# A two-layer kernel with an order written by a planner: 40 instead of 42 dense chunks ahead of the routing, and gathered rows added five steps behind their request

## The chip, the cores and the metric

The kernel runs on one core of one Trainium2 chip. Engines are called PE (TensorE, matrix products; PEld is its weight load), DVE (VectorE), ACT (ScalarE), POOL (GpSimd) and SP (SyncE, which here only issues DMAs). The metric is the device time of one execution in microseconds, as the median of several runs. Everything is computed in 32-bit floats.

## The reference

Four sequences of 512 tokens with 256 features (2048 tokens) go through two layers. Each layer normalises x, and adds an attention-like and a feed-forward branch to x.

```
xn = layernorm(x)
x  = x + attn0(xn) + ffn0(xn)
     attn0: q, k, v = xn Wq, xn Wk, xn Wv (+ biases);  phi = elu + 1
            ((phi(q) * cumsum(phi(k) * v)) / 4) Wo + bo           # sum along the sequence
     ffn0:  logits over 512 genes, top 32, softmax, weighted mean of gene vectors,
            tanh(mean Wd) * rms(xn) * (mean Wu) * 0.1
xn = layernorm(x)
x  = x + attn1(xn) + ffn1(xn)
     attn1: q, k, v = rms(xn) Wqkv;  q, k = rms(q), rms(k);  w = exp(k)
            y = sigmoid(q) * cumsum(w * v) / (cumsum(w) + 1e-6)
            xn + (u * silu(g)) Wout   with u, g = y Wswiglu      # width 1024
     ffn1:  16 experts of width 176, top 2 by softmax, weighted;
            plus a shared expert of width 352
```

## The kernel before

**Stages.** (1) The *planned stage*, 0 to 295 us: all of layer 0 and, in layer 1, everything up to `y` and the router's choice. It works in five *units*: the two halves of batch 0 (units 0 and 1, 256 tokens each), then batches 1, 2 and 3 (units 2, 3 and 4, 512 tokens each). (2) *Routing*: `route` works out, for each token and choice, the row (`slot`) at which the token is stored for its expert, then `scatter` writes the tokens' rows to `xrows` in device memory by 32 indirect DMAs of POOL. (3) The *expert stage*, 363 to 463 us: 19 pairs of 128-row tiles are fetched, turned, multiplied with their expert's weights (`up_tile`, `down_pair`) and stored to `yrows`. (4) The *last stage*: the rows of each token are gathered back by 32 indirect DMAs of POOL (L1610), multiplied with the choice's weight and added to x by DVE (L1621), and x is stored.

**Dense chunks.** The rest of layer 1 (the product of `y` with the wide weights, and the shared expert) is filler for TensorE, cut into 88 *chunks*: 8 halves of a batch (256 tokens), each with 11 blocks of hidden units (3 of the shared expert, 8 of attention). A chunk is an up product into a PSUM tile `gu` (L1163), a tanh on ACT (`th`), two multiplications that make `hid`, and a down product that adds to `acc` (L1184), which has a single buffer. After a half's last block `sum_up` (L1196, DVE) adds `acc` to x and so frees it. Chunks `0 .. UPTO-1` run in the planned stage, five beside `route`, 18 beside `scatter`, three more before the experts, and all others in the last stage. There the down product of a chunk follows the up product of the one two later (`behind`). Each indirect DMA is *paced*: it waits for the latest down product (`beat`).

**The planner.** In the planned stage the order of instructions of PE, DVE, ACT and POOL is not that of the program text. Work is written as generators that yield what they need next: an engine with an estimated duration, a buffer (`take`, `give`), or an event (`wait`, `post`). `Order.run` keeps a clock for each engine and picks among the steps that could begin within `PULL[engine]` of the earliest the one with the lowest rank. `RANKS` has a rank for each kind of work and unit. Each engine then executes its list in that fixed order. Outside the planned stage a scheduler orders the instructions by their place in the text and by dependences.

**Lean choices.** `LEAN` says, for each unit, which engine does a step. `rise`: whether the gene branch's product is made by ACT and POOL (L626, L629) instead of DVE (L634). `value`: whether `v` is scaled by ACT (L861) instead of DVE (L867). `begin`: whether layer 1's normalisation (L374, called from `begin_stream`) runs on POOL instead of DVE. `inverse`, of effect only in units of 512 tokens: whether one reciprocal of 256 columns (L966) serves two columns at once, with POOL multiplying before (L962) and after it (L978, L979) and the last product in the form L981 instead of L990. `dense`: chunks below this number have `hid` made by an ACT copy (L1240) and a POOL multiplication (L1243); the others by a DVE multiplication (L1246). `norm` and `taken` belong to layer 0 and are the same in both kernels.

**Chain of a unit in layer 1.** `begin_stream`: moments and factors (DVE, L361 to L371, L812 to L814), normalisation (L374), transposes (PE, L380); an addition of `xn` to x on POOL (L822). `rest_stream`: products with the weights `w1` (PE, L877), squares and exponentials (ACT), then for each of two heads of columns `gate_stream`: a transpose, a running sum (DVE, L933), the product L953, reciprocals (L966), another transpose and running sum, and the product that makes `yT` (L990 or L981). The wide chunks of a batch need its `yT`.

**The last stage's loop** steps once per chunk. The requests, the adds and the stores of it:

```
for step, _ in enumerate(dd):
    while asked < 2 * NTT and 5 * asked <= 9 * step:          # gather a row block (POOL)
    while added < 2 * NTT and 15 * added <= 32 * (step - 3):  # add one (DVE), store each fourth (SP)
```

With `NTT` = 16 there are 32 requests and 32 adds; `NT` = 4 tiles of 128 tokens make a batch.

Of the kernel before, what the change touches and what calls it, by code (L numbers as in the profile page):

```python
# [17 lines left out]
P = 128  # L18
B, L, D = 4, 512, 256
NT = L // P  # L20
# [8 lines left out]
NTT = B * NT  # L29
# [20 lines left out]
def together(*streams):  # L50
# [9 lines left out]
PE, DVE, ACT, POOL = "PE", "DVE", "ACT", "POOL"  # L60
# [1 line left out]
REACH = {PE: 0.2, DVE: 0.13, ACT: 0.15, POOL: 0.1}  # L62


PULL = {PE: 0.2, DVE: 0.02, ACT: 0.05, POOL: 0.1}

RANKS = dict(
    front=(-12, 14.5, -21, -10.5, -7.5),  # L70
    turn=(-35, -36, -36, -36.5, -31.5),
    logit=(10.5, 14, 25.5, 28, 26),
    top=(-11.5, 16, 15.5, 16.5, 26),
    gene=(-46.5, -21, -41.5, -40, -30.5),
    kv=(-2, 21.5, -7.5, -8.5, 17.5),
    q=(37.5, 43, 41.5, 50, 43),
    out=(-23.5, -22.5, -5.5, -6.5, -15),
    begin=(-23.5, -26.5, -27.5, -17.5, -15.5),
    rest=(9, -28.5, -9, 4.5, -27),
    weigh=(51.5, 51, 51.5, 50.5, 52.5),  # L80
    gate=(3.5, 4, -1.5, 4.5, 9.5),
    router=(32.5, 34, 26.5, 29, 33.5),
    dense=(49, 9.5, 2),
)


# [18 lines left out]

LEAN = dict(
    taken=(1, 0, 1, 1, 1),
    rise=(0, 0, 1, 0, 0),
    norm=(0, 1, 1, 1, 1),
    value=(1, 0, 1, 1, 0),  # L110
    inverse=(1, 1, 1, 0, 0),
    begin=(0, 1, 1, 0, 1),
    dense=27,
)


class Order:
# [67 lines left out]
    def run(self):  # L185
        while self.live:
# [6 lines left out]
            if not self.live:  # L193
# [6 lines left out]
                for j, (s, t) in enumerate(zip(ready, begin))  # L200
                if s.ask[0] == engine and t <= begin[first] + PULL[engine]
            ]
# [12 lines left out]
def tile_two_layers(  # L215
# [23 lines left out]
    nc = tc.nc  # L239
# [5 lines left out]
    xs = const.tile([P, B, NT, D], F32, name="xs")  # L245
# [911 lines left out]
    NC = len(chunks)  # L1157
# [13 lines left out]
    def source(half):  # L1171

        unit = (half // 2, half % 2 * 2)
        return (unit, 0) if unit in made else ((half // 2, 0), half % 2 * HB)
# [19 lines left out]
    def sum_up(half):  # L1194
        here = xs[:, half // 2, half % 2 * 2 : half % 2 * 2 + 2]
        V.scalar_tensor_tensor(here, acc, 0.5, here, ALU.mult, ALU.add)  # L1196

    def dense(first, behind):

        for c in range(first, 2 * B * NC):
            half, n = divmod(c, NC)
            unit, t0 = source(half)
            m = chunks[n][4]
            gu = ps_d.tile([P, 2, HB], F32, name="gu")
            up_product(gu, made[unit], t0, *chunks[n])
            th = wd.tile([P, HB], F32, name="th", bufs=3)
            S.activation(th[0:m], gu[0:m, 0], AF.Tanh, scale=0.5)  # L1209
            hid = wd.tile([P, HB], F32, name="hid", bufs=4)  # L1210
            V.scalar_tensor_tensor(th[0:m], th[0:m], 1.0, gu[0:m, 0], ALU.add, ALU.mult)  # L1211
            V.tensor_tensor(hid[0:m], gu[0:m, 1], th[0:m], ALU.mult)
            behind.append((half, n, hid))
            if len(behind) > 2:
                half, n, hid = behind.pop(0)
                down(half, n, hid)
                if n == NC - 1:
                    sum_up(half)
            yield
        for half, n, hid in behind:  # L1220
            down(half, n, hid)
        sum_up(half)
# [93 lines left out]
    def weight_stream():  # L1316
# [10 lines left out]
        for transfer in incoming:  # L1327
            paced(transfer)
            c += 1
            if c < UPTO:  # L1330
                yield "wait", ("down", c)

    UPTO = 42
    kinds = mybir.EngineType
    with tc.manual_schedule(engines={kinds.PE, kinds.DVE, kinds.Activation, kinds.Pool}):

# [15 lines left out]
        order.add(more_constants(), RANKS["front"][0])  # L1352
        dense_streams(order, UPTO)
        for unit, (b, i0, nt) in enumerate(((0, 0, 2), (0, 2, 2), (1, 0, NT), (2, 0, NT), (3, 0, NT))):
# [5 lines left out]
        order.run()  # L1360
    mixing.close()
    dd = dense(UPTO, [])

    def d(n):
# [240 lines left out]
    added = 0  # L1605
    for step, _ in enumerate(dd):
        while asked < 2 * NTT and 5 * asked <= 9 * step:
            n, k = divmod(asked, 2)
            paced(
                G.indirect_dma_start(  # L1610
                    out=ys[:, asked],
                    out_offset=None,
                    in_=yrows,
                    in_offset=bass.IndirectOffsetOnAxis(ap=slot[:, k, n : n + 1], axis=0),
                ).ins
            )
            asked += 1
        while added < 2 * NTT and 15 * added <= 32 * (step - 3):
            n, k = divmod(added, 2)
            here = xs[:, n // NT, n % NT]  # L1620
            V.scalar_tensor_tensor(here, ys[:, added], cpair[:, k, n : n + 1], here, ALU.mult, ALU.add)  # L1621
            added += 1
            if added % 4 == 0 and added < 2 * NTT:
                b, i = divmod(n - 1, NT)
                nc.sync.dma_start(
                    out[b, i * P : (i + 2) * P].rearrange("(t p) d -> p t d", p=P), xs[:, b, i : i + 2]
                )
    assert asked == added == 2 * NTT
    for i in (NT - 2, NT - 1):
        nc.sync.dma_start(out[B - 1, i * P : (i + 1) * P], xs[:, B - 1, i])  # L1630

# [54 lines left out]
```

## Time and profile before

| | us |
|---|---|
| median of 3 runs (lowest to highest) | 526.89 (526.8 to 528.15) |
| the profiled execution | 527.08 |
| its span on the core | 525.4 |

| stage of the profiled execution | from, to |
|---|---|
| planned stage, to the first product of the routing | 0 to 296.06 |
| routing, scatter, 26 dense chunks | 296 to 363 |
| experts | 363 to 463 |
| last stage, to the first of the last two stores | 463 to 520.46 |
| those stores, and the end of the program | 520.46 to 525.4 |

Busy time is a share of the span; matrix products are pipelined, so that a busy PE is not a PE at its peak, but a gap in it is time in which no product was under way. In a timeline row stand start, duration, engine, line, operation, written tile `<-` read tiles, shapes and count; in brackets the engine's idle time just before and what ended it.

### The profile page before, as it was taken

The numbers are of one execution on the slowest core, as the hardware profiler recorded it, in microseconds if no ns is written. First come the engines' busy times: TensorE is split into PE (matmuls) and PEld (weight loads), VectorE is DVE, ScalarE is ACT, GpSimd is POOL, SyncE is SP. The second block draws the span as 40 slices with busy tenths as digits, with TensorE's granted clock in tenths as the row PEclk, the third lists the DMA queues.
The fourth block names the chain that finished last, engine by engine and source line by source line (L and its number), as shares of the span: only waits on it lengthen the run. The fifth ranks groups of instructions, "written<-read, shape, count | busy, mean of one in ns | idle before, by whom it ended". The sixth has DMA issues, their size and how long they took to land.

```text
span 525.4 us, 7219 instructions
## 1 busy us (share of the span) xinstructions
PE 506.4 (96%) x2352; PEld 371.8 (71%) x2352; DVE 346.5 (66%) x938; ACT 238.0 (45%) x539; POOL 197.7 (38%) x229
## 2 busy tenths in 40 slices
PE   7899999999999999999899999999999999999895
PEld 5555575565676787678578888887776767688784
DVE  5899989999899799859559783333222222226653
ACT  2864896668757845873381111113333333311110
POOL 1713076364745566477220126660000000026562
PEclk8999999999999999999999999999999999999998
DMA  7999000000000000006516203245237345114442
GB/s 213 351 378 327 1 1 1 1 1 2 0 1 1 1 1 1 1 1 181 151 48 183 100 30 139 92 185 182 88 100 289 102 154 196 61 61 130 130 122 83
DMA packets 38920, 53.71 MB, mean 102 GB/s; under 512 B 4096, under 2 KB 33888, under 8 KB 38624
## 3 DMA queue, kind: packets, MB, share of 16 engines
q1 hardware_dynamic: 35104, 44.82, 25.2%
q0 software_dynamic: 3072, 8.39, 4.9%
q8 instruction: 20, 0.33, 0.3%
q14 instruction: 20, 0.16, 0.1%
q10 hardware_dynamic: 704, 0.01, 0.1%
HBM read 27.12 MB, written 18.61 MB: 87 GB/s over the span
## 4 chain that ended last, share of the span: by engine, by line
PE 62%; DVE 17%; POOL 8%; issue 5%; ACT 3%; DMA 2%; SPq 0%; POOLq 0%; ACTq 0%; DVEq 0%
PE gu L1163 16%; PE pu L1461 9%; PE acc L1184 8%; PE py L1483 6%; PE pm L877 6%; POOL ys L1610 5%; PE pm L413 4%; PE pt L1414 3%; PE pm L456 3%; DVE rep L560 3%; DVE top L558 2%; PE pm L380 2%; DVE sums L966 1%; PE pm L483 1%; PE pm L489 1%
## 5 line engine op out<-in xcount | busy, mean ns | idle before, releaser
L1163 PE MATMUL gu<-yT,wugt 128*128 128x256 f32 x512 | 120.4, 379 | 0.0
L1163 PEld LDWEIGHTS gu<-yT,wugt 128*128 128x128 f32 x512 | 96.3, 190 | 13.4 <-issue 0.8
L1610 POOL DMA_INDIRECT ys<-yrows,slot x32 | 30.5, 952 | 129.1 <-PE gu L1163 111.9
L1184 PE MATMUL acc<-wot,hid 128*128 128x256 f32 x256 | 66.0, 383 | 2.3 <-DVE hid L1246 1.4
L1209 ACT ACTIVATE th<-gu 128x256 f32<-128x256 f32 (+1 forms) x46 | 17.6, 383 | 103.9 <-PE gu L1163 61.6
L1184 PEld LDWEIGHTS acc<-wot,hid 128*128 128x128 f32 x256 | 47.1, 190 | 11.9 <-DVE hid L1246 2.9
L1163 PE MATMUL gu<-xn1T,sgu 128*128 128x256 f32 (+1 forms) x192 | 45.4, 380 | 0.0
L1461 PE MATMUL pu<-wex,xgT 128*128 x128 | 43.6, 463 | 1.8 <-issue 1.0
L877 PE MATMUL pm<-w,xn1T 128*128 128x512 f32 (+1 forms) x128 | 45.2, 495 | 0.0
L1211 DVE SCALAR_TENSOR_TENSOR th<-th,gu 128x256 f32<-128x256 f32 (+1 forms) x46 | 19.1, 415 | 39.1 <-ACT th L1209 27.8
L1470 DVE TENSOR_TENSOR hb<-pu,hb 128x176 f32<-128x176 f32 x38 | 13.0, 341 | 43.8 <-ACT hb L1469 43.8
L1138 POOL DMA_INDIRECT xrows<-xn,slot x32 | 31.0, 967 | 28.0 <-DVE hit L1118 11.2
L374 POOL TENSOR_SCALAR xn<-xs,mv,rs 128x256 f32<-128x256 f32 x24 | 29.3, 1233 | 27.8 <-DVE rs L754 21.1
L1163 PEld LDWEIGHTS gu<-xn1T,sgu 128*128 128x128 f32 (+1 forms) x192 | 34.5, 181 | 7.2 <-issue 1.0
L413 PE MATMUL pm<-xnT,wqkv 128*128 128x512 f32 x72 | 33.9, 598 | 0.0
L877 PEld LDWEIGHTS pm<-w,xn1T 128*128 128x128 f32 x128 | 23.5, 190 | 14.4 <-issue 10.7
L558 DVE MAX8 top<-rep 128x8 f32<-128x512 f32 x48 | 32.8, 683 | 0.3
L560 DVE MATCH_REPLACE8 rep<-top,rep 128x512 f32<-128x512 f32 x48 | 32.4, 675 | 0.0
L456 PE MATMUL pm<-wct,xnT 128*128 128x512 f32 x64 | 31.8, 620 | 0.3 <-ACT lg L517 0.2
L1474 DVE COPY hgT<-pt 128x512 f32<-128x512 f32 x19 | 13.1, 692 | 28.6 <-PE pt L1414 28.6
L1483 PE MATMUL py<-wex,hgT 128*128 x128 | 30.6, 382 | 0.0
L1233 ACT ACTIVATE th<-gu 128x256 f32<-128x256 f32 (+1 forms) x42 | 16.0, 383 | 31.9 <-PE gu L1163 30.8
(205 smaller groups left out, 946.6 us busy)
## 6 DMA issues: line engine op xcount, KB each, us to landing
xrows<-zero SPq DMA_DIRECT2D x1, 6016.0 KB
wex<-in_w_gate_up_dram SPq DMA_DIRECT2D x8, 704.0 KB, 5.0
xn<-wex SPq DMA_DIRECT2D x9, 608.0 KB, 4.3
xg<-xrows SPq DMA_DIRECT2D x19, 256.0 KB, 2.8
yrows<-yg SPq DMA_DIRECT2D x19, 256.0 KB, 2.1
wugt<-in_wug_dram SPq DMA_DIRECT2D x1, 2048.0 KB
wex<-in_w_down_dram SPq DMA_DIRECT2D x4, 512.0 KB
w<-wex SPq DMA_DIRECT2D x3, 608.0 KB
```

The lines of the kernel that those rows point to most:

```text
L374: engine.tensor_scalar(to, xs[:, b, i], mv[:, 0:1], rs[:, 0:1], ALU.subtract, ALU.mult)
L413: T.matmul(pm, wqkv[:, h, c * P : (c + 1) * P], k.xnT[:, h, tok], start=(h == 0), stop=(h == NH - 1),)
L456: T.matmul(pl, k.xnT[:, h, i * P : (i + 1) * P], wct[:, h], start=(h == 0), stop=(h == NH - 1))
L558: V.max(tp[:, 8 * r : 8 * r + 8], src)
L560: V.match_replace(rep, tp[:, 8 * r : 8 * r + 8], src, TAKEN)
L877: T.matmul(po[:, 0:n], g.xnT[:, h, i * P : (i + 1) * P], w1[:, h, 0:n] if o == "q" else w1[:, h, 2 * D : 2 * D + n], start=(h == 0), stop= ...
L1138: sc = G.indirect_dma_start(out=xrows, out_offset=bass.IndirectOffsetOnAxis(ap=slot[:, k, i : i + 1], axis=0), in_=xn1[:, i // NT, i % NT] ...
L1163: T.matmul(gu[0:m, k], w[:, h, at : at + m], ins[which][:, h, t0 : t0 + HB], start=(h == 0), stop=(h == NH - 1),)
L1184: mm = T.matmul(acc[:, t], hid[0:m, t * P : (t + 1) * P], dw[0:m, dc], start=(n == 0 and t == 0), stop=(n == NC - 1), skip_group_check=True,)
L1461: T.matmul(pg[rows, 0 : 2 * NI], pairs[p]["xT"][:, i, h, rows], w[:, bass.ds(at + h * 2 * NI, 2 * NI)], start=(h == 0), stop=(h == NH - 1),)
L1483: mm = T.matmul(py[rows, i * D : (i + 1) * D], hT[:, i, h, rows], w[:, bass.ds(at + EW - (2 - h) * D, D)], start=(h == 0), stop=(h == 1),)
L1610: G.indirect_dma_start(out=ys[:, asked], out_offset=None, in_=yrows, in_offset=bass.IndirectOffsetOnAxis(ap=slot[:, k, n : n + 1], axis=0) ...
```

## The change

`UPTO` goes from 42 to 40, so that two dense chunks move from the planned stage to the last one, which then has 22 steps; the chunks beside the routing keep their number (26) but are chunks 40 to 65. Requests keep their pace. Adds go out two a step, for the first time in step 6. In the last step no down product is issued with the up product; the three that are left come after the loop, and so behind that step's adds in the text. Of the last two stores the second is issued from ACT's queue. In the planned stage, ranks, one `PULL` and several lean choices are new.

```diff
-PULL = {PE: 0.2, DVE: 0.02, ACT: 0.05, POOL: 0.1}
+PULL = {PE: 0.2, DVE: 0.02, ACT: 0.05, POOL: 0.2}
 RANKS = dict(
-    front=(-12, 14.5, -21, -10.5, -7.5),
-    turn=(-35, -36, -36, -36.5, -31.5),
-    logit=(10.5, 14, 25.5, 28, 26),
-    top=(-11.5, 16, 15.5, 16.5, 26),
-    gene=(-46.5, -21, -41.5, -40, -30.5),
-    kv=(-2, 21.5, -7.5, -8.5, 17.5),
-    q=(37.5, 43, 41.5, 50, 43),
-    out=(-23.5, -22.5, -5.5, -6.5, -15),
-    begin=(-23.5, -26.5, -27.5, -17.5, -15.5),
-    rest=(9, -28.5, -9, 4.5, -27),
-    weigh=(51.5, 51, 51.5, 50.5, 52.5),
-    gate=(3.5, 4, -1.5, 4.5, 9.5),
-    router=(32.5, 34, 26.5, 29, 33.5),
-    dense=(49, 9.5, 2),
+    front=(-15.5, 16, -19, -12, -6),
+    turn=(-35.5, -35, -36, -37.5, -39.5),
+    logit=(25, 14.5, 22, 35.5, 26),
+    top=(-13, 14.5, 15, 12.5, 24),
+    gene=(-45.5, -21.5, -41.5, -39, -32.5),
+    kv=(-1.5, 22, -10.5, -9.5, 18),
+    q=(38.5, 39.5, 42.5, 42.5, 42.5),
+    out=(-25.5, -24, -9.5, -22, -13),
+    begin=(-15, -27, -16.5, -14, -11),
+    rest=(8.5, -23, -10.5, 5.5, -28),
+    weigh=(53, 54, 51.5, 53, 50.5),
+    gate=(7, 4, -1.5, 7.5, 5.5),
+    router=(32.5, 34, 25, 30, 34.5),
+    dense=(49, 9, 2.5),
 )
 LEAN = dict(
     taken=(1, 0, 1, 1, 1),
-    rise=(0, 0, 1, 0, 0),
+    rise=(0, 0, 1, 0, 1),
     norm=(0, 1, 1, 1, 1),
-    value=(1, 0, 1, 1, 0),
-    inverse=(1, 1, 1, 0, 0),
-    begin=(0, 1, 1, 0, 1),
-    dense=27,
+    value=(1, 1, 1, 0, 0),
+    inverse=(0, 1, 1, 1, 1),
+    begin=(0, 1, 1, 0, 0),
+    dense=18,
 )
...
             behind.append((half, n, hid))
-            if len(behind) > 2:
+            if len(behind) > 2 and c < 2 * B * NC - 1:
                 half, n, hid = behind.pop(0)
                 down(half, n, hid)
...
-    UPTO = 42
+    UPTO = 40
...
-        while added < 2 * NTT and 15 * added <= 32 * (step - 3):
+        while added < 2 * NTT and added < 2 * (step - 5):
...
-    for i in (NT - 2, NT - 1):
-        nc.sync.dma_start(out[B - 1, i * P : (i + 1) * P], xs[:, B - 1, i])
+    for i, queue in ((NT - 2, nc.sync), (NT - 1, nc.scalar)):
+        queue.dma_start(out[B - 1, i * P : (i + 1) * P], xs[:, B - 1, i])
```

## The prediction

> **What bounds the kernel now.** I read the page first for the engines' shares, then the table by stage (busy time in stretches cut at the stages' ends) for TensorE's idle time, then the timeline at the few places where TensorE waits.
>
> ```profile
> PE 506.4 (96%) x2352; PEld 371.8 (71%) x2352; DVE 346.5 (66%) x938; ACT 238.0 (45%) x539; POOL 197.7 (38%) x229
> ```
>
> ```profile
> 14.00:60.00 46.00, 43.69 (x168) 25.93 (x167) 44.11 (x114) 32.65 (x61) 15.92 (x16) 1.00 0.84 299
> ...
> 200.00:240.00 40.00, 39.57 (x207) 28.50 (x206) 32.49 (x112) 28.08 (x75) 26.49 (x32) 1.00 0.05 13
> 240.00:256.00 16.00, 14.59 (x72) 11.92 (x71) 15.72 (x24) 5.48 (x9) 8.88 (x8) 1.00 0.68 197
> 256.00:276.00 20.00, 20.00 (x79) 14.20 (x78) 8.81 (x42) 13.81 (x36) 2.80 (x4) 1.00 0.22 70
> 276.00:295.40 19.40, 19.40 (x101) 16.69 (x99) 18.00 (x24) 2.30 (x6) 0.00 (x0) 1.00 0.61 189
> 295.40:363.00 67.60, 66.91 (x311) 57.98 (x310) 32.09 (x92) 9.93 (x26) 32.73 (x38) 1.00 0.30 115
> ...
> 463.00:520.50 57.50, 54.57 (x251) 46.72 (x249) 30.42 (x74) 8.25 (x21) 30.45 (x32) 1.00 0.38 112
> ```
>
> After the stretch's length come the busy times of PE, PEld, DVE, ACT and POOL, then the granted clock. The clock is 1.00 throughout, and PE is idle for 2.31 + 0.43 + 1.41 us in the rows shown and 0.34 + 0.07 in those left out (60 to 100 and 150 to 200), together 4.6 us, between 14 and 295.4, the planned stage after its start-up; for 0.7 us in routing and scatter; and for 2.9 us in the last stage. So TensorE sets the time nearly everywhere. The change adds and removes no matrix product. It can win little more than these 7.5 us and something of the 4.9 us after the last product; it can lose whatever TensorE is made to wait. VectorE is the second engine: 15.7 of 16 us in 240 to 256 and 18.0 of 19.4 in 276 to 295.4.
>
> The last stage's waits are these (the bracket is the idle time before, and its releaser):
>
> ```profile
> 493.79 0.48 DVE L1621 SCALAR_TENSOR_TENSOR xs<-ys,cpair,xs 128x256 f32<-128x256 f32 x1 [1.26 <-DMA ys<-yrows,slot]
> ...
> 494.53 0.68 DVE L1196 SCALAR_TENSOR_TENSOR xs<-acc,xs 128x512 f32<-128x512 f32 x1
> ...
> 495.27 0.70 PE L1184 MATMUL acc<-sdn,hid 128*128 128x256 f32 x2 [1.54 <-DVE xs L1196]
> ...
> 517.70 0.48 DVE L1621 SCALAR_TENSOR_TENSOR xs<-ys,cpair,xs 128x256 f32<-128x256 f32 x1 [0.51 <-DMA ys<-yrows,slot]
> 518.10 0.42 DVE L1212 TENSOR_TENSOR hid<-gu,th 128x256 f32<-128x256 f32 x1
> ...
> 518.57 1.13 PE L1184 MATMUL acc<-wot,hid 128*128 128x256 f32 x4 [0.58 <-DVE hid L1212]
> ```
>
> Twice VectorE stands at an add whose gathered rows have not landed, what TensorE needs queues behind it, and TensorE stops: 1.54 us of idle time for `sum_up` at the boundary of two halves (acc has one buffer), and 0.58 us for the last chunk's `hid`.
>
> **Part 1: the last stage.** Successive `gu` groups start 2.59 us apart there (511.78 and 514.37 in the timeline): the price of a chunk, 12 product records. Two more chunks cost 2 x 2.59 = 5.2 us here and take the same 5.2 us from the planned stage: zero, if the planned stage really ends that much earlier (part 3).
>
> Adds now run two a step from step 6 to step 21; requests keep their pace and end at step 18. Add a runs at step 6 + a/2 and its request went out at step 5a/9, so the distance is six steps at first and three at the end: at least 7.8 us, where a request issued at 468.03 fed an add at 471.14, 3.1 us later. The 19.6 us that the adds wait for DMA in all should go. What is late next: in a full step VectorE has 2 x 0.48 + 0.42 + 0.42 = 1.8 of 2.59 us, so it keeps up, but `sum_up` can still sit behind one add. Of the boundary stop I take 1.4 us of 1.54 as won, of the last stop 0.5 of 0.58, since one of the two adds of the last step may still stand ahead of the last `hid`. Sum -1.9 us. If all adds stay in front: -0.9.
>
> Last downs: from 514.37 TensorE already runs the last up product and then eight down products from 516.09, the order that the new condition writes down. VectorE's last adds have no request beside them. I cost this at 0; hidden by the 1.73 us of two down groups, and if the order did change, at most one group of 0.87 us either way.
>
> Last two stores: SP issues them 0.40 us apart (520.46 and 520.86 in the trace). Its waits for their landing clear at 523.49 and 523.67, 0.18 us apart. The Trainium skill ("Trainium Kernel Development and Optimization", Key Constraints) says that issuing DMAs from several engines saves only the sequencer's issue time: that would be 0.40. I take the row, -0.2. On ACT the load of `need` and a branch (0.5 us) now queue behind the store's wait; the store's own 3.0 us to landing covers them, and without that cover they would cost 0.5. SP is passed by one store, POOL's requests are not moved.
>
> **Part 2: lean choices in the planned stage**, with mean durations by line. Nine chunks (18 to 26) lose an ACT copy (0.38) and a POOL multiply (0.75) and gain a VectorE multiply (0.40): DVE +3.6, ACT -3.4, POOL -6.8. Pair inversion for the last two batches takes one of two reciprocals per head: 4 x 1.74 = -7.0 on DVE, +1.0 for `yT` in the L981 form (0.94 against 0.69), and 12 POOL multiplies of 0.73: +8.8. `begin` of the last batch: four POOL normalisations of 1.23 (-4.9) become four of 0.42 on DVE (+1.7). `rise` there: -1.9 DVE, +2.9 POOL, +1.9 ACT. `value`: two tiles leave DVE, four come: +0.9. The two moved chunks: -1.6 DVE. Sums: DVE -3.3, POOL 0.0, ACT about -3. These lie beside TensorE's work; they count only through the chain of part 3. PULL and RANKS add no instruction: they reorder all five engines' queues up to 290 us. Nothing in the trace prices an order. Gain: at most the 4.6 us of idle time. Loss: bounded by part 3's price, 5.2 us. I take 0.
>
> **Part 3: can the last batch come 5.2 us earlier?** With two chunks fewer as filler, TensorE reaches the last batch's transposes 5.2 us sooner; what these read must be ready as much sooner.
>
> ```profile
> 250.05 2.36 POOL L822 TENSOR_TENSOR xs<-xs,xn 128x1024 f32<-128x1024 f32 x1
> 250.16 2.79 DVE L990 TENSOR_TENSOR yT<-sums 128x512 f32<-128x512 f32 x1
> ...
> 253.34 1.13 PE L1184 MATMUL acc<-wot,hid 128*128 128x256 f32 x4 [1.36 <-DVE hid L1246]
> ```
>
> For: the four normalisations hold POOL from 245.14 to 249.97, and on DVE take 1.7 us: -3.1. The factors that they read, at 242.44, stand behind two reciprocals of batch 2, of which one goes: -1.7. The last batch's two heads lose two reciprocals: -3.5. Against: the nine multiplies, +3.6. Sum -4.7, half a microsecond short of 5.2.
>
> Here a rule speaks against the change. The yT row took 2.79 us in place of the 0.69 of its neighbours because POOL's addition had begun 0.1 us before; the next `hid`, at 252.88, came behind it, and TensorE paid 1.36 us of idle time. The Trainium skill ("SBUF — State Buffer", Who interferes with whom) says that a DVE instruction with two SBUF inputs and a POOL instruction that reads SBUF exclude each other, and the second waits for all of the first. This row shows just that. The new POOL multiplies stand right ahead of the two-input `yT` products: by the rule each of the four could wait a whole multiply, 4 x 0.73 = 2.9 us. By the L981 rows, the same pattern in batch 1 (0.68 and 1.20), it is 0.25 each, 1.0 us, already counted. I take the rows, since each `yT` needs the multiplies' results and only another head's can meet it. The shortfall of 0.5 stands against the 1.36 us stop above, which an earlier normalisation moves and may dissolve: net 0 for the planned stage.
>
> **Sum** against the profiled execution (527.08 us; span 525.4 and 1.7 around it): -1.9 - 0.2 + 0 = 525.0. The median of the runs shown, 526.89, is 0.2 lower: **524.8 us**.
>
> **The rivals.**
> A (chance 0.45): as summed, 524.8, between 523.6 and 525.2.
> B (0.17): the new order also removes 2.5 of the planned stage's 4.6 us, as the relief of DVE (88% busy from 14 to 295) would allow: 522.3; all of it would be 520.2. Against it: the idle time is scattered, and 2.3 us of it lie before 60, where no lean choice changes.
> C (0.25), slower: the last batch is late. DVE takes the normalisations in turn behind batch 2's scans and wins nothing there, so -3.1 becomes 0; then -1.7 - 3.5 + 3.6 = -1.6 of the 5.2 needed, and TensorE waits 3.6 us before the last transposes; with the exclusion at its full price (2.9 - 1.0) it is 5.5 us. That gives 524.8 + 3.6 = 528.4 to 530.3. It decides once the last batch is more than 2.1 us late; 3.7 us makes it slower by 0.3%. For it: DVE at 15.7 of 16 us around 250. Against it: VectorE is idle for 11 of 20 us between 256 and 276, so delays before 256 can be made up only in ACT's and TensorE's parts of the chain.
> D (0.13): the two cancel, 526.5; or the change does not do what it says, adds still waiting since the scheduler orders them otherwise.
>
> **How the numbers follow.** A change of 0.3%, 1.6 us, is about what a measurement here can tell from none. Faster needs under 525.3: A and B, 0.62. Within: D and the mild end of C, 0.15. Slower by over 0.3% (over 528.5): the rest of C, 0.23. The range for 8 in 10 runs from 520.8, most of B, to 529.8, most of C; A's own range is 523.6 to 525.2.
>
> **What would show it.** Right: the adds' wait for DMA falls from 19.6 us to under 2; no idle time of over 0.5 us before acc at the half boundary or the last group; the last stage is 5.2 us longer than before less 2, and the first routing product at about 291 in place of 296.06. L966 has four records fewer, L1243 nine. Wrong: PE idle of over 5 us between 240 and the first routing product, behind DVE `sums` or `xn`, or `yT` rows over 1.5 us; that is C. A prediction under 522 fails if the idle time before 60 is unchanged and that at 240 to 256 stays.

## The result, and the profile after

The changed kernel takes **530.88 us** (median of 6 runs, 530.16 to 532.23), beside 527.69 us for the kernel before on the same chip: ratio 1.0065, 95% interval 1.0046 to 1.0085. It is 0.65% slower, where 524.8 us was predicted, 2.1 us less than the kernel before. The profiled execution took 530.16 us with a span of 528.3, 2.9 more than before. Line numbers from about 1220 on are one higher than before.

The engines' shares and the granted clock, from the page:

```profile
PE 506.4 (96%) x2352; PEld 372.6 (71%) x2352; DVE 342.9 (65%) x945; ACT 237.1 (45%) x532; POOL 198.0 (37%) x232
...
PEclk9999999999999999999999999899999999999999
```

TensorE's busy time is in sum what it was, so by the totals the 2.9 us are idle time. But one slice behind the middle has a lower clock, and there products take longer. The table by stretches says where (columns: length, busy PE, PEld, DVE, ACT, POOL, then the granted clock):

```profile
240.00:260.00 20.00, 20.00 (x97) 16.35 (x96) 16.13 (x36) 7.47 (x15) 10.68 (x10) 1.00 0.59 180
...
320.00:340.00 20.00, 16.93 (x77) 14.32 (x76) 6.41 (x15) 2.68 (x7) 12.34 (x14) 0.98 0.29 115
340.00:360.00 20.00, 20.00 (x88) 17.34 (x88) 5.82 (x14) 2.57 (x7) 8.18 (x9) 0.94 0.47 171
```

The planned stage is sound: around 250, where the kernel before had a stop of 1.36 us and where rival C expected a long one, TensorE has none. It waits 1.31 us (before: 0.62) just ahead of the routing. The idle time is in the stage of the scatter: 3.07 us between 320 and 340, and the clock falls to 0.94 behind it. In the kernel before routing and scatter together had 0.7 us. The timeline at that place:

```profile
332.17 1.03 PE L1184 MATMUL acc<-wot,hid 128*128 128x256 f32 x4
333.03 1.89 PE L1163 MATMUL gu<-xn1T,sgu 128*96 128x256 f32 x8
336.04 0.38 ACT L1209 ACTIVATE th<-gu 128x256 f32<-128x256 f32 x1 [5.88 <-PE gu L1163]
...
336.46 0.42 DVE L1211 SCALAR_TENSOR_TENSOR th<-th,gu 128x256 f32<-128x256 f32 x1 [5.39 <-issue]
...
336.92 0.42 DVE L1212 TENSOR_TENSOR hid<-gu,th 128x256 f32<-128x256 f32 x1
337.26 0.68 DVE L1196 SCALAR_TENSOR_TENSOR xs<-acc,xs 128x512 f32<-128x512 f32 x1
...
337.99 1.13 PE L1184 MATMUL acc<-sdn,hid 128*128 128x256 f32 x4 [3.07 <-DVE xs L1196]
...
338.96 3.53 PE L1163 MATMUL gu<-yT,wugt 128*128 128x256 f32 x8
```

Read it from the bottom up. The first down product of chunk 55 (the first chunk of half 5) waits 3.07 us for `acc`, which has one buffer and is freed by `sum_up` (L1196). The last down product of half 4 had ended by 333.2, so `sum_up` could have run then. VectorE executes in order, and ahead of it stood the two multiplies of chunk 56, whose tanh began only at 336.04. The last record of its up product had begun at 331.95 and ended 0.38 us later: the tanh is 3.71 us late. After the idle time the next up product takes 3.53 us for eight records in place of 1.89. The price is 3.07 + 1.64 = 4.7 us. The granted clock, 1.00 on either side of this stretch, accounts for the second part: 3.4 us at half speed cost 1.7.

```profile
339.05:342.45 3.40, 3.40 (x10) 2.65 (x9) 0.00 (x0) 0.00 (x0) 1.16 (x2) 0.50 0.29 116
```

In the kernel before the same place looks like this; there the tanh of chunk 56 was 0.7 us late, the one of chunk 57 2.4 us, and its multiplies stand behind `sum_up`:

```profile
333.73 0.38 ACT L1209 ACTIVATE th<-gu 128x256 f32<-128x256 f32 x1 [2.88 <-PE gu L1163]
334.14 0.42 DVE L1211 SCALAR_TENSOR_TENSOR th<-th,gu 128x256 f32<-128x256 f32 x1 [2.38 <-issue]
...
334.94 0.68 DVE L1196 SCALAR_TENSOR_TENSOR xs<-acc,xs 128x512 f32<-128x512 f32 x1
335.68 1.13 PE L1184 MATMUL acc<-sdn,hid 128*128 128x256 f32 x4
...
338.04 0.38 ACT L1209 ACTIVATE th<-gu 96x256 f32<-96x256 f32 x1 [3.93 <-PE acc L1184]
```

The last stage, for comparison with the lines shown of before:

```profile
497.67 0.48 DVE L1622 SCALAR_TENSOR_TENSOR xs<-ys,cpair,xs 128x256 f32<-128x256 f32 x1
...
498.40 0.68 DVE L1196 SCALAR_TENSOR_TENSOR xs<-acc,xs 128x512 f32<-128x512 f32 x1
...
499.14 1.13 PE L1184 MATMUL acc<-sdn,hid 128*128 128x256 f32 x4 [1.20 <-DVE xs L1196]
...
519.97 2.75 PE L1184 MATMUL acc<-wot,hid 128*128 128x256 f32 x12
...
523.48 0.35 SPq L1631 DMA_DIRECT2D out_dram<-xs  x1
523.48 0.37 ACTq L1631 DMA_DIRECT2D out_dram<-xs  x1
```

The last stop is gone (the last three down products run as one row of twelve records); the one at the border of halves is 1.20 us, and the adds still wait for their rows: each of the 32 begins 2.7 to 3.7 us after its request, as before (2.7 to 3.6). From the list of waits:

```profile
DVE xs L1622 <- DMA ys<-yrows,slot: 17.8, 24, 1.4
...
PE acc L1184 <- DVE xs L1196: 4.5, 3, 3.1
```

As a sum: at equal work (the up product of chunk 57) the changed kernel is 0.7 us ahead of the one before, at that of chunk 65 it is 4.0 behind, so 4.7 went in between. The experts take 0.2 longer. From the last `py` product to TensorE's end it takes 59.32 - 55.34 = 4.0 us more for two chunks of 2.59, a gain of 1.2. From the first of the last two stores to the end 4.86 us pass in place of 4.90. 4.0 + 0.2 - 1.2 = 3.0, the 2.9 of the rounded spans.

### The profile page after: what moved, and what is told of

The parts are those of the page before. It is cut to its first block, busy times and chain, and to the rows that moved or that the text cites. A ratio compares the mean times of both kernels' runs of the same rounds, so it can differ in the third digit from the quotient of the medians.

```text
span 528.3 us, 7221 instructions
## 1 busy us (share of the span) xinstructions
PE 506.4 (96%) x2352; PEld 372.6 (71%) x2352; DVE 342.9 (65%) x945; ACT 237.1 (45%) x532; POOL 198.0 (37%) x232
## 4 chain that ended last, share of the span: by engine, by line
PE 65%; DVE 20%; issue 6%; POOL 6%; DMA 2%; ACT 1%; SPq 0%; POOLq 0%; DVEq 0%; ACTq 0%
PE gu L1163 20%; PE acc L1184 11%; PE pu L1462 9%; PE py L1484 6%; PE pm L877 6%; PE pt L1415 3%; DVE rep L560 3%; DVE top L558 3%; POOL ys L1611 3%; PE pm L380 2%; PE pm L456 2%; DVE phi L430 2%; DVE cum L442 1%; PE pm L413 1%; DMA xs<-in_x_dram 1%
## 5 line engine op out<-in xcount | busy, mean ns | idle before, releaser
L1163 PE MATMUL gu<-yT,wugt 128*128 128x256 f32 x512 | 122.7, 383 | 0.0
L1209 ACT ACTIVATE th<-gu 128x256 f32<-128x256 f32 (+1 forms) x48 | 18.3, 383 | 113.4 <-PE gu L1163 77.1
L374 POOL TENSOR_SCALAR xn<-xs,mv,rs 128x256 f32<-128x256 f32 x20 | 24.5, 1234 | 26.2 <-DVE rs L754 21.4
L541 POOL TENSOR_TENSOR e<-e,rep 128x512 f32<-128x512 f32 x14 | 18.0, 1290 | 37.0 <-ACT rep L538 37.0
```

What stands on the lines that cost most here:

```text
L374: engine.tensor_scalar(to, xs[:, b, i], mv[:, 0:1], rs[:, 0:1], ALU.subtract, ALU.mult)
L1163: T.matmul(gu[0:m, k], w[:, h, at : at + m], ins[which][:, h, t0 : t0 + HB], start=(h == 0), stop=(h == NH - 1),)
```

## The experiments

First theory (T1): the loss is one stop, made by a late tanh and handed on by VectorE's order. Rivals: the new ranks and lean sums cost it; 40 chunks do, however the rest lies; the late tanh was a chance of one profile. "Stop" is TensorE's wait before chunk 55's first down product in the profiled execution, "late" what the tanh of chunk 56 was late there. Each group of experiments ran on another chip, with the kernel before beside it (527.8 us in the first two groups, 526.9, 526.1 and 526.1 in the others), so compare ratios across groups and times within one.

| group | kernel | us, median | ratio (95%) | stop | late |
|---|---|---|---|---|---|
| 1 | e1, as changed, again | 530.85 | 1.006 (1.0041 to 1.0079) | 2.51 | 3.15 |
| 1 | e2, sum first | 525.16 | 0.9956 (0.9939 to 0.9974) | 0 | 0 |
| 1 | e3, no scatter | 525.52 | 0.9956 (0.9943 to 0.9969) | 0 | 0 |
| 1 | e4, old ranks, 40 chunks | 531.02 | 1.0058 (1.0037 to 1.008) | 2.71 | 3.35 |
| 2 | e5, new ranks, 42 chunks | 524.83 | 0.994 (0.9921 to 0.9959) | 0.51 | 0.91 |
| 2 | e6, adds tied | 528.77 | 1.0016 (1.0003 to 1.0029) | 3.19 | 3.83 |
| 2 | e7, sum first, adds tied | **523.87** | 0.9917 (0.9895 to 0.994) | 0 | 0.44 |
| 2 | e8, before with sum first | 526.97 | 0.9981 (0.9972 to 0.9991) | 0.36 | 0.77 |
| 3 | e11, scatter two chunks later | 529.31 | 1.0065 (1.004 to 1.009) | 0.40 | 0.80 |
| 3 | e12, e7 with 42 chunks | 524.55 | 0.9956 (0.9943 to 0.9969) | 0.43 | 0.83 |
| 5 | e16, sum first at one border | 524.04 | 0.9959 (0.9946 to 0.9971) | 0 | 0 |
| 5 | e17, third scatter earlier | 523.87 | 0.9952 (0.9936 to 0.9968) | 0 | 0 |
| 5 | e18, e17 with adds tied | 523.43 | 0.9948 (0.993 to 0.9965) | 0 | 0 |

Read the last two columns together: the stop goes with the lateness of this one tanh, in every row.

**e1: again.**

> The changed kernel once more, nothing edited. Theory: its loss is one stop in the stage of the scatter, at the border of halves 4 and 5. There ScalarE began the tanh of chunk 56 3.71 us after its up product was done; VectorE takes its work in order and had that chunk's multiply ahead of the sum of the half, so TensorE waited 3.07 us for the one acc buffer and then ran the next up product in 3.53 us where 1.89 is usual. If this belongs to the kernel: TensorE waits 2 to 3.5 us before chunk 55's first down product again, and the time is 530 to 532. Rival, the late start was a chance of that one profile: the wait there is under 1 us, and as the time of the runs without profile is the same 530.9, the loss has to be elsewhere.

The stop is there, and all four runs lie between 530.52 and 531.43. The chance of one profile is out.

**e2: the sum ahead of the gating.** In `dense`, for every chunk after the routing:

```diff
+            summed = None
+            if len(behind) > 1 and c < 2 * B * NC - 1:    # down product and sum of the chunk two earlier
+                ...
+                    summed = sum_up(half)
             S.activation(th[0:m], gu[0:m, 0], AF.Tanh, scale=0.5)
-            V.scalar_tensor_tensor(th[0:m], ...)
+            gated = V.scalar_tensor_tensor(th[0:m], ...)
+            if summed is not None:
+                tc.add_manual_dep(gated.ins, summed.ins.name, <same engine, order only>)
```

> The changed kernel with the down product and the sum of a half put ahead of the next chunk's gating in the code of the dense chunks, and the gating's first VectorE instruction tied behind the sum, in the stages after the routing too. Theory (a late start on ScalarE, handed on by VectorE's order): the sum no longer stands behind chunk 56's multiply, so TensorE does not wait before chunk 55's first down product (under 0.5 us, before: 3.07) and the slow up product after it (1.64 us more than usual) goes too: 530.9 - 4.7 = 526.2, and up to 1.2 less if the wait at the border of halves in the last stage goes as well, so 525 to 526.2. The late starts on ScalarE themselves should stay. Rival, the stop only moves to the three gu buffers: TensorE waits as long before the up product of chunk 59, and the time stays at 530 to 531.

Measured 525.16. At the border (L1217 is the tanh here, L1219 the first multiply):

```profile
332.30 1.03 PE L1184 MATMUL acc<-wot,hid 128*128 128x256 f32 x4
...
333.36 0.69 DVE L1196 SCALAR_TENSOR_TENSOR xs<-acc,xs 128x512 f32<-128x512 f32 x1 [2.00 <-PE acc L1184]
...
334.88 1.03 PE L1184 MATMUL acc<-sdn,hid 128*128 128x256 f32 x4
...
338.88 0.39 ACT L1217 ACTIVATE th<-gu 128x256 f32<-128x256 f32 x1 [3.42 <-PE acc L1184]
```

The first down product of the next half has no bracket: no wait. Late tanhs are still there (chunks 50, 54, 58, 62, up to 2.70 us). The time lies in T1's range, if 1.0 us under the 526.2 that it gives without a gain at the border in the last stage; from the up product of chunk 57 to the experts' first product its profile shows 23.3 us, that of the changed kernel 28.3. Yet the run does not prove T1: chunk 56's tanh was not late in it. The edit also moved one down product at the border of halves 3 and 4, which let the third scatter start 1.3 us earlier, and with it the late starts moved. Order or place is taken up by e16 and e17. The border in the last stage still costs 1.2 us, as an add stands in the way:

```profile
PE acc L1184 <- DVE xs L1632: 1.2, 1, 1.2
```

**e3: no scatter.** `together((scatter(), 33), d(18))` becomes `run_all(d(18)[0])`.

> The changed kernel without the scatter of the rows to the experts' order (left out; the experts then work on rows that were never written), the 18 dense chunks beside it run alone. Theory that the late starts on ScalarE come with the scatter's transfers: from the routing to the experts no tanh begins over 1 us after its up product, TensorE waits under 0.5 us before chunk 55's first down product, and that stretch is 4.5 to 5 us shorter: about 526. Rival, ScalarE is late for a reason of its own: the late starts of 1.7 to 3.7 us stay, and the time stays within 1 us of 530.9.

No stop, and not one late tanh between the routing and the experts. They come with the scatter.

**e4: the old ranks with 40 chunks**, and **e5: the new ranks with 42.** e4 puts back `RANKS`, `PULL[POOL]` and the changed entries of `LEAN`. e5:

```diff
-    UPTO = 40
+    UPTO = 42
-        while added < 2 * NTT and added < 2 * (step - 5):
+        while added < 2 * NTT and 15 * added <= 32 * (step - 3):
```

> The changed kernel with the ranks, the pull of POOL and the list of lean sums of the kernel before; 40 chunks, the adds and the last stores stay as changed. Theory (one stop in the scatter's stage, where the ranks have no part): the planned part costs about what the changed one does (within 1.5 us), and the stop at chunk 55's first down product decides the rest: 2 to 3 us of it, 530 to 532, if the late starts fall as in the changed kernel; 526 to 527 if they fall on other chunks. Rival, the new ranks and lean sums cost it in the planned part: the first routing product comes over 2 us earlier than 293.15, and the time falls to 526 to 528 with the stop still in place.

> The changed kernel with 42 chunks up to the routing and 20 steps in the last stage, as in the kernel before, and that kernel's rule for when a gathered row is added; the changed ranks, lean list and last stores stay. The scatter then begins two chunks later against the border of halves 4 and 5 than with 40. Theory (a late start on ScalarE costs only where it falls on the chunk just ahead of a sum): the late starts stay (1.7 to 4.2 us, a few chunks apart), but as in the kernel before they miss chunk 56, TensorE waits under 1 us before chunk 55's first down product, and the time is 526 to 528. Rival, it is the changed ranks and lean sums that bring the stop: 2.5 to 3 us of waiting there again and 530 or more.

Crossed like this, stop and time follow 40 or 42 and not the ranks. The new ranks and lean sums are a gain: e5 is 3.0 us faster than the kernel before, more than the 526 to 528 expected. In its profile the first routing product begins at 293.59, before at 296.06, behind as many down products and two more up records: 2.5 us come from the planned stage. The profiled execution, at 527.12 us one of the two slowest of eight, lost 2.2 us again in the last stage, where 1.90 us of idle time at the border were followed by a granted clock of 0.50. The faster six were not profiled; their granted clocks over the whole run are higher (0.993 to 0.998 in place of 0.990).

**e6: the adds really late.** `paced(...)` around the add makes it wait for the latest down product issued ahead of it.

> The changed kernel with each add of a gathered row tied to the last down product issued ahead of it in the code, so that the instruction scheduler can no longer move it up behind its request. Theory (the adds never were five steps behind, the scheduler moved them up): VectorE's wait for gathered rows falls from 17.8 us to under 2, the wait of TensorE at the border of halves in the last stage falls from 1.20 to under 0.5 us, and as the stop beside the scatter stays, the time is 529.7 (530.9 less 1.2). Rival, VectorE waits for the down product now in place of the row and holds the gating up as long: the wait at the border stays at 1.2 us or more, and the time at 530.9 or above.

VectorE's wait for gathered rows is gone from the list of waits, and no idle time over 0.45 us is left at the border in the last stage. In its place stands only this:

```profile
DVE xs L1622 <- PE acc L1184: 0.7, 2, 0.5
```

So "five steps behind" had never been in force: without a dependence the scheduler put each add right behind its request. In e6 the adds begin 5.5 to 15.3 us after it, in the changed kernel 2.7 to 3.7. The median of 20 runs is 528.77 (526.31 to 531.19) and not 529.7; the profiled one, at 530.52, had the full stop beside the scatter. Times so far apart, at granted clocks of 0.987 to 1.000, suggest that the stop is not equally long in each execution; only one was profiled.

**e7: both edits.**

> The changed kernel with both edits: the sum of a half ahead of the next chunk's gating, and the adds tied to the down products. Theory: the two stops are apart and their prices add: the 4.7 us beside the scatter, which the first edit alone has won (525.2 measured), and 1.2 us at the border in the last stage, where that edit left 1.21 us because two adds stood ahead of the sum: 524.0. Rival, the last stage's stop moves on (the tied adds pile up ahead of the last sum, whose add and store then end later): 525 to 526.

As expected: with the first stop gone, the second edit wins another 1.3 us (525.16 to 523.87). This version beats both kernels, by 0.83% the one before. Its border in the last stage:

```profile
491.39 0.69 DVE L1196 SCALAR_TENSOR_TENSOR xs<-acc,xs 128x512 f32<-128x512 f32 x1 [0.59 <-PE acc L1184]
...
492.91 1.03 PE L1184 MATMUL acc<-sdn,hid 128*128 128x256 f32 x4
```

**e8: the same sum first on the kernel before.**

> The kernel before with the sum of a half put ahead of the next chunk's gating, as in the second experiment. Theory (there the late start fell on chunk 57, behind the sum, and cost 0.23 us only): nothing to win beside the scatter, and in the last stage at most the 1.54 us at the border, if no add stands ahead of the sum: 526 to 527.7, over 0.5 us above the changed kernel with the same edit (525.2), so that the rest of the change is worth that much once the border is safe. Rival, the edit is a gain of its own, whatever the change: the kernel before with it takes 525.2 or less.

A gain of 0.8, at the border in the last stage (0.46 us of idle time for 1.54). The edit is no gain of its own.

**e11: the scatter two chunks later.** `d(5)` beside the routing becomes `d(7)`, and two chunks fewer run alone.

> The changed kernel with seven in place of five dense chunks beside the routing, so that the scatter runs beside chunks 47 to 64 and not 45 to 62, as in the kernel before; 40 chunks ahead of the routing and all else as changed. Theory (the stop is a coincidence of the scatter's place with the border of halves): the 10th scatter falls at chunk 52 and the next late starts at 56 to 57 or later, TensorE waits under 1 us before chunk 55's first down product, and the time is 526 to 527. Rival, the stop belongs to 40 chunks however the scatter lies: 2.5 to 3 us there and 530 to 531.

Half right. The stop falls to 0.40 us with 40 chunks and VectorE's old order: it depends on where the scatter lies. The time is no better, since the scatter now ends right ahead of the experts, whose first rows it writes:

```profile
359.71 0.63 PE L1415 MATMUL pt<-ident,xg 128*128 128x128 f32 x4 [2.82 <-DMA xg<-xrows]
361.11 2.58 PE L1462 MATMUL pu<-wex,xgT 128*128 x4 [0.78 <-DMA xg<-xrows]
```

2.82 us of waiting, and behind it four `pu` records take 2.58 us, where the same four took 1.45 in e2.

**e12: e7 with 42 chunks** and the add's rule of before.

> The sum of a half ahead of the gating and the adds tied to the down products, with the changed ranks and lean sums, but 42 chunks ahead of the routing, 20 steps in the last stage and the add's rule of the kernel before. Theory (with the border safe 40 and 42 chunks differ little): the changed ranks with 42 took 524.8, in whose profile TensorE waited 0.51 and 1.90 us at the two borders; without these 522.5, with 0.3 to 0.5 us back for adds that stand ahead of the last sum: 522.5 to 523.5, so up to a microsecond better than the same with 40 chunks (523.9). Rival, 40 chunks are the better number: 524.5 or more.

Not the 522.5 to 523.5 expected: by that rule two adds stand ahead of the last `hid`, and TensorE waits 1.44 us for it.

**What holds the tanh.** Beside the scatter the late starts fell at the 10th to 12th, 17th to 21st, 24th to 26th and 31st request. The next five kernels were run once each, e9 and e10 in group 3, e13 to e15 in group 4.

e9, every second scatter left out (`if i % 2: yield; continue`):

> The changed kernel with every second of the 32 scatters left out (half of the experts' rows are then never written), the others at their places. In the runs so far the late starts of ScalarE fell at the 10th to 12th, 17th to 21st, 24th to 26th and 31st scatter, whatever the chunk. Theory (they count scatters): of 16 scatters only the 10th, near chunk 55 or 56, brings one group of late starts, and there are none around the others. Rival (they come by time, every four to five chunks): three or more groups, four to five chunks apart, as with all 32. The time alone does not tell these apart, as a late start near chunk 56 can bring the stop again.

525.21, and no late tanh beside the scatter. Neither theory said so. POOL now sends one request in 2.59 us on average and rests between them, but there are also only half as many:

```profile
328.27 0.96 POOL L1141 DMA_INDIRECT xrows<-xn,slot  x1 [1.63 <-PE acc L1187]
```

e10, six copies `S.copy(tick[0:m, k], gu[0:m, 0, 0:8])` behind each tanh:

> The changed kernel with six small copies (8 columns of gu) on ScalarE behind each tanh of the chunks from 40 to 65, none of which waits for another engine. What is ScalarE late for? Theory A (the engine itself stands still): the late starts stay at the 10th, 17th to 21st, 24th to 26th scatter, and some begin inside a row of copies, as a gap of over 1 us between two of them. Theory B (the instruction fetch of ScalarE falls behind): with seven times the instructions there are clearly more groups of late starts than the three or four of the changed kernel. Theory C (only the wait of the tanh for its semaphores is answered late): all late starts lie ahead of a tanh, none inside the copies, and their count stays.

There are five groups of late starts in place of three or four, each ahead of a tanh and none inside the copies. That speaks against A; but the copies cover under a quarter of the time, and between B and C it does not decide. With more work in it the kernel took 527.07 us (526.9 for the kernel before on that chip), less than the changed one elsewhere (530.9): its late starts fell on chunks 54 and 57 and left the border alone.

e13, a copy of eight columns of `gu` on VectorE ahead of each tanh:

> The changed kernel with a small copy on VectorE (8 columns of gu) of each up product of the chunks from 40 to 65, which waits for TensorE alone, as the tanh does but for its free buffer. Theory A (ScalarE is held): the copy of a chunk begins within 0.3 us of its up product's end while the same chunk's tanh begins 1 to 4 us late. Theory B (TensorE's signal itself comes late): the copy begins as late as the tanh, within 0.2 us of it, in each late group, where VectorE was free before. The copy can also stand behind a multiply that waits for the tanh of the chunk before; only chunks where VectorE had nothing ahead of it count.

529.53 us, with a stop of 2.40 us. The run speaks for theory B, and against T1 as first put. In the four groups with VectorE free beforehand (chunks 50, 51, 56, 62) its copy, which waits for TensorE alone, began 1.08, 3.48, 2.79 and 2.07 us after the up product's end, and the tanh 0.2 us behind it each time. For chunk 51, whose up product ended at 319.33:

```profile
322.81 0.17 DVE L1211 COPY seen<-gu 128x8 f32<-128x8 f32 x1 [3.49 <-PE acc L1184]
323.00 0.39 ACT L1212 ACTIVATE th<-gu 128x256 f32<-128x256 f32 x1 [4.60 <-issue]
```

Two engines see the same product late, while TensorE goes on. Then `sum_up`, which waits for TensorE too, can be late by itself. e12 shows it: VectorE has been free for 3.53 us when the sum begins, 1.40 us after the down product (330.49 + 1.03) had ended.

```profile
330.49 1.03 PE L1184 MATMUL acc<-wot,hid 128*128 128x256 f32 x4
...
332.92 0.69 DVE L1196 SCALAR_TENSOR_TENSOR xs<-acc,xs 128x512 f32<-128x512 f32 x1 [3.53 <-PE acc L1184]
...
333.67 1.13 PE L1184 MATMUL acc<-sdn,hid 128*128 128x256 f32 x4 [0.43 <-DVE xs L1196]
```

And at a lateness of 0.8 to 0.9 us the stop is 0.36 and 0.43 us with the sum first (e8, e12), 0.51 and 0.40 without (e5, e11): at this size VectorE's order makes no difference.

e14, 64 of 128 rows in each scatter (`slot[0:64, ...]`, `xn1[0:64, ...]`):

> The changed kernel with each of the 32 scatters moving 64 of its 128 rows (the other half of the experts' rows is left unwritten). Theory A (the late starts come from the traffic, which falls behind at 128 rows every 1.4 us): none over 1 us beside the scatter, TensorE waits under 0.5 us before chunk 55's first down product, about 525.5. Theory B (they come from the number of requests): the groups at the 10th, 17th to 21st and 24th to 26th scatter stay.

Late starts of 3.02, 2.47, 2.13 and 1.47 us stay, at the 10th, 19th, 26th and 32nd request. It is the requests, not the rows they move. 526.34 us (before: 526.07): they fell on chunk 55, the tanh of chunk 56 was 1.40 us late, and the stop was 0.76 us.

e15, scatters not tied to the down products (`paced(sc)` taken out):

> The changed kernel with the scatters no longer tied to the down products, so that POOL issues them as fast as it can (1.26 us each, some 41 us in all in place of 47). Theory A (requests that come faster than they land hold ScalarE): groups of late starts come closer together, three chunks apart or less, until about 40 us after the first scatter, and none later. Theory B (POOL's and ScalarE's waits for TensorE's signals hold each other up): without POOL's waits no tanh is over 1 us late and the stop is gone, about 526.

551.8 us, further than theory A went. In the changed kernel, too, requests go out 1.27 us apart, but there a late signal holds POOL up as well: the 3rd to the 12th from 309.30 to 320.69, the 13th only at 323.84, behind the late tanh of chunk 51; the 13th to the 21st to 333.95, then that of chunk 56. Here nothing stops them: the tanh of chunk 51 comes 19.5 us late, and TensorE stands still for 13.6 us (L1208 is the tanh, L1183 the down product):

```profile
338.98 0.96 POOL L1138 DMA_INDIRECT xrows<-xn,slot  x1 [0.30 <-issue]
339.18 0.39 ACT L1208 ACTIVATE th<-gu 128x256 f32<-128x256 f32 x1 [17.18 <-remote]
...
340.54 2.07 PE L1183 MATMUL acc<-wot,hid 128*128 128x256 f32 x4 [13.62 <-issue]
```

The second theory (T2), then: requests of POOL that follow each other closely for long make the other engines see TensorE's products late; where that falls on the border of two halves, `acc` comes free late and TensorE stops.

**e16 to e18: order or place.** The edit of e2 for one chunk only, in place of all: e16 at the border of halves 4 and 5 (`if c == 56:`; TensorE's order as in the changed kernel), e17 at that of halves 3 and 4 (`if c == 45:`; VectorE's order at 4/5 the old one, the third scatter earlier). e18 ties the adds in e17.

> The changed kernel with the sum ahead of the next chunk's gating for chunk 56 alone (the border of halves 4 and 5); TensorE's order stays that of the changed kernel, and so does the scatters' start. Theory A (VectorE's order makes the stop): sum_up begins at the down product's end, TensorE waits under 0.5 us before chunk 55's first down product, 526.2 (530.9 less 4.7). Theory B (TensorE's signal is late for VectorE too): sum_up itself waits with VectorE free, until about when the late tanh begins; only the 0.8 to 1.2 us of the two multiplies go, the stop is 1.5 to 2.5 us, the clock still falls for part of it, and the time is 528.5 to 530.

> The changed kernel with the sum ahead of the next chunk's gating for chunk 45 alone (the border of halves 3 and 4, ahead of the scatters); VectorE's order at the border of halves 4 and 5 stays the old one, with chunk 56's multiplies ahead of the sum. TensorE's order changes by one down product there, which lets the third scatter start 1.3 us earlier. Theory A: the stop stays at 2.4 to 3.2 us, 530 to 531. Theory B: the late signals come after the 10th, 17th and 24th scatter and miss the border, as in the sum-first kernel; the stop is under 0.5 us and the time 525 to 526.

> The previous kernel with the adds tied to the down products. If VectorE's order has no part in the gain (theory B): the same 523.9 as with the sum first everywhere and the adds tied, within 0.7. If it has (theory A): 528 to 529, as with the adds tied alone.

They do not decide it. All three profiles on this chip have not one late start after the routing, at the scatter or at the gathers. Yet the first twelve scatters of e16 stand 0.06 to 0.07 us ahead of those of the changed kernel, and its 3rd to 17th follow each other without a pause; the first ten of e17 stand 0.11 to 0.12 us ahead of those of e2, which had its first late tanh there. So close requests alone do not make signals late: something else, perhaps of the chip, has a part. The numbers of e17 and e18 fit "place", that of e16 neither theory as put; without late starts both orders should give the same, and do (524.0 and 523.9). What e17 does show: where nothing is late, VectorE's old order costs nothing.

```profile
332.18 1.03 PE L1184 MATMUL acc<-wot,hid 128*128 128x256 f32 x4
332.38 0.38 ACT L1217 ACTIVATE th<-gu 128x256 f32<-128x256 f32 x1 [2.21 <-PE gu L1163]
...
333.59 0.68 DVE L1196 SCALAR_TENSOR_TENSOR xs<-acc,xs 128x512 f32<-128x512 f32 x1
...
334.77 1.03 PE L1184 MATMUL acc<-sdn,hid 128*128 128x256 f32 x4
```

**What stays open.** How much VectorE's order adds to a stop when the signal is over 3 us late: in the changed kernel `sum_up` began 1.2 us after the tanh, so by T2 it is at most that much of the 3.07 us, but no run isolates it. Whether the changed kernel would have had its stop on the last chip: it was not run there. Whether 32 requests with pauses between them would cost nothing: e9 has pauses, but also half the requests. What carries the delay from POOL's requests to the other engines: no record shows a signal on its way, and in e15 TensorE also pauses up to 2 us inside one up product, where nothing is waited for, so that signals may not be all that is late. The fetch of instructions by DMA is a rival that the traces speak against: its two queues moved nothing from 306.3 to 331.2 us in the changed kernel, in which time chunks 51 and 52 were late, nor from 306.4 to 346 in e15.

## Why the prediction was wrong, step by step

**What failed: a term that was not in the sum.** Routing and scatter had 0.7 us of idle time and were left out as a place where little could be won. But taking two chunks out of the planned stage moves the scatter by two chunks against the halves, and late starts came to lie on a border: +4.7 us, of which the other steps won back 1.7. "What is late next" was asked for the adds, and whether work is ready in time for the last batch, but neither for this stage. The trace of before had the sign, a tanh 2.4 us late one chunk behind the border. None of the rivals named it; rival C gave the right side for a wrong reason.

**Part 1, -1.9:** measured -1.2. The last stop went (0.58). "The 19.6 us that the adds wait for DMA in all should go" failed: 17.8 were left, and the boundary stop stayed at 1.20 of 1.54, because outside the planned stage the text's order binds nobody: the distance of "at least 7.8 us" was 2.7 to 3.7. Rival D had said so in half a sentence, without a price. With a dependence (e6) it went as the step said.

**Last two stores, -0.2:** not seen. SP and ACT do issue together, at 523.48, but the end comes only 0.04 us sooner behind that. **Last downs, 0:** as said.

**Part 2:** in the planned stage DVE's busy time fell by 4.1 us (3.3 predicted), POOL's by 0.1 (0), ACT's by 0.8 (3, though the terms listed for ACT make only 1.5). The six `yT` products of L981 took 0.69 us each, less than the 0.94 of the rows that were taken: no multiply of POOL held one up. The 0 taken for the new order was too low: with 42 chunks the changed ranks and lean sums bring the routing 2.5 us forward (e5), as much as rival B had named at a chance of 0.17 for 40.

**Part 3, net 0:** better than that. The first routing product came at 293.15 and not at 291, but behind as many up records as before (338) and eight down records fewer (1.73 us): at equal work 2.9 - 1.7 = 1.2 us sooner. Rival C's idle time before the last transposes is not there.

## What to carry to other kernels

When a change shifts one stage against another, look in the old trace for near misses in the stages that it does not edit: a signal that came late one chunk behind a single-buffered tile was the stop of the new kernel. Be wary of indirect DMAs that POOL issues for long without a pause while other engines exchange short steps; that pauses alone cure it was not tested. And an order that must hold has to be a dependence, for a scheduler may undo what the text says.

## What the runs showed of the hardware

Beside indirect DMAs of POOL, ACT and DVE started late on products that TensorE had finished: not at all at one request in 2.59 us (e9), by 1 to 4 us where up to ten requests in a row stood 1.2 to 1.3 us apart and a late signal then stopped them, by 19 us at one per 1.27 us that nothing stopped (e15). This was so in the experiments on four chips, and not in the three kernels (e16 to e18) on the fifth.

A short rest is dear. After idle times of 1.90 to 3.19 us (e5 in the last stage; e13, e1, e4, the changed kernel and e6 beside the scatter) TensorE lost another 1.6 to 1.8 us in the next twelve records, with a granted clock of 0.50; after 1.20 to 1.75 us (the longest in e13, ahead of the routing) it did not. In e1:

```profile
338.18 1.82 PE L1184 MATMUL acc<-sdn,hid 128*128 128x256 f32 x4 [2.51 <-DVE xs L1196]
339.80 2.93 PE L1163 MATMUL gu<-yT,wugt 128*128 128x256 f32 x8
342.56 1.03 PE L1184 MATMUL acc<-sdn,hid 128*128 128x256 f32 x4
343.43 1.89 PE L1163 MATMUL gu<-yT,wugt 128*128 128x256 f32 x8
```

1.82 for 1.03 and 2.93 for 1.89. The Trainium skill ("TensorE: Matmul & The Clock Gate", Part 1: The HAM clock gate) has the clock halved after an idle window of about 3.4 us; here 1.90 us of idle time was enough. By the page the stop would have cost 3.07 us, by the runs it was 4.7.
